# A graph and expert megakernel on one Trainium2 core: ten groups instead of six added back in the slots, another spacing of gathers and sorting steps, and attention's sum on GpSimd

## The chip, the cores and the metric

The kernel runs on 1 core of one Trainium2 chip. The metric is the device time in microseconds (us) of that core for one execution. The engines are named as in the profile: PE is TensorE's matmul, PEld its load of weights, DVE is VectorE, ACT is ScalarE, POOL is GpSimd and SP is SyncE, which here only issues DMAs.

## The reference

The input is `x`, 128 x 64 rows of 256 features (8192 tokens), with an adjacency matrix of 64 x 64 for each of the 128 graphs. Two layers follow one another, each with a part over the graph and a feed-forward part (FFN), and each part is added to `x`:

```python
x = x + _L0_gnn_ref(_layernorm(x), adj, ...)
x = x + _L0_ffn_ref(_layernorm(x), ...)
x = x + _L1_gnn_ref(_layernorm(x), adj, ...)
x = x + _L1_ffn_ref(_layernorm(x), ...)

def _L0_ffn_ref(...):                       # one expert of eight for each token
    H = gelu(xf @ W1 + b1)                  # 1024 hidden features
    probs = softmax(H @ Wg + bg); assign = argmax(probs)
    for e in range(8):
        y = H @ Wd[e] + bd[e]
        out = out + where(assign == e, probs[:, e] * y, 0.0)

def _L1_gnn_ref(...):                       # attention inside each graph
    Wh = h @ W
    e = leaky_relu((Wh @ a1)[:, :, None] + (Wh @ a2)[:, None, :], 0.2)
    attention = softmax(where(adj > 0, e, NEG))
    h_prime = attention @ Wh
    return gelu(layernorm(h_prime) * gamma + beta)
```

The first graph part is a convolution with the normalised adjacency and a softplus. The last FFN takes gates from attention over 1,048,576 edges (a softmax of all the edges that end in a token), chooses 2 of 4 experts with them, and runs experts of 512 hidden features. Everything is float32 at the borders.

## The kernel before, in words

The 8192 tokens are 64 tiles of 128 tokens by 256 features, and they stay in SBUF as `x` (128 x 64 x 256, one tile is `x[:, t, :]`). Four tiles make a group (`GR = 4`), two groups a part (`PART = 2`). The program is written as generators that are advanced in turn, and a scheduler fixes the order of the instructions on each engine when the program is built: it takes what is ready by its own estimate, and `tc.issue_after(i)` holds what is emitted under it back until instruction `i` has its place. `reuse_waits="tile"` makes the next user of a buffer wait for the users of the one before.

The stages, by the profiled execution:

- *0 to about 655 us*: the first graph part and the hidden features of the first FFN. The tokens are ordered by their expert, and their hidden rows are written to DRAM in that order (`hrows`).
- *Slots, 655 to 918* (`slots`, from L1297 on, and the loop L1399 to L1413). A slot is 128 tokens of one expert. SP issues a DMA transpose that loads its hidden rows as `hTt`; TensorE adds the bias with a first matmul (L1340) and multiplies with 8 pieces of the expert's weights as 16 instructions (L1348); ScalarE copies the result from PSUM (L1356) and sends it to DRAM (`yrows`, L1357). The loop runs 60 slots.
- Beside each slot the loop advances three generators. `counts` (`Keys.count`, L328) counts the edges by the token that they end in: VectorE makes a pair of one-hot arrays with one comparison each (L209, 128 x 2048 and 128 x 1024 elements) and TensorE multiplies them into `cnt_ps` (L348). `steps` (`Keys.finish`, L360) sorts the edges' keys on VectorE in small steps, and each `next(steps)` takes one. `back_early` (`back_first`, L1268) adds the FFN's rows back to `x`: GpSimd gathers the 128 rows of a tile from `yrows` into `yearly` (L1285, an indirect DMA; five buffers, `HELD + 2`), and after `HELD` = 3 more gathers VectorE multiplies the tile by its probability and adds it to `x` (L1276), then takes the statistics for the next layernorm (L1277, bn_stats). The gather of tile `t` is emitted once the number of slots done reaches that in L1282; which slots hold a tile's rows depends on the data, so it waits for the stores emitted before it. When a part's eight tiles are in, `factors_of` (L245) makes the layernorm's scale and mean for the parts that attention needs first.
- *Attention, 920 to 1246* (loop L1733 to L1769, steps `s` = 4 to 25, a group advances by one stage in a step). The streams of a step are `back` (L1563: four gathers L1569 into `yin`, additions L1584, statistics L1561), `combine` (L1669), `tables` (L1687), `second` (L1642) and `first` (L1604), and each works on another group: group `s - 4` has its scores made in `first` (transposes, matmuls, `ee` at L1627), group `s - 5` its softmax and product in `second`, group `s - 7` is finished in `combine`, and group `s - 10` gives its rows for the edges in `tables`. `back` runs for `s >= BACKED` alone, since the groups below were added in the slots; their statistics come from `raws1`. After each second step `make_factors` (L1715) turns the statistics of the two groups that were added back, of the two rows of products and of the two finished groups into factors.
- The order of `back` in attention: the additions L1584 of groups 2 to 4 wait for a place behind the last factors, those of groups 5 to 8 behind the last scores, and later ones are free (`ahead` in `back`). Its `yin` buffers (six) are also those of the experts' `y`.
- `combine` ends with two instructions of VectorE for each tile (L1674, L1675), a gelu of the whole group on ScalarE (L1679, 128 x 1024), the sum `x + gelu` on VectorE (L1682, 128 x 1024) and the statistics of the sum for the last layernorm. There are 16 of each. Expert units of the last FFN (L1490 and L1500) fill in from `s` = 12 on.
- *1246 to 1951*: the edges' softmax and gates, and the experts, with matmuls of TensorE nearly throughout.

GpSimd also copies while the first stage runs (L598, 64 x 256 elements), which the prediction uses for its price, as it does the short `guess` instructions of VectorE (L163).

Of the kernel before, what the change touches and what calls it, by code (L numbers as in the profile page):

```python
# [17 lines left out]
ALU = mybir.AluOpType  # L18
# [9 lines left out]
PART = 2  # L28
# [6 lines left out]
SURE = 68  # L35
EARLY = 8
AHEAD = 3
BACKED = 3 * PART
HELD = 3
COUNTED, HE = 6, 8  # L40
EPS = 1e-5
# [46 lines left out]
def kernel(  # L88
# [31 lines left out]
    nc = tc.nc  # L120
    V, S = nc.vector, nc.scalar
    FD = f0_w1.shape[1]
    NH = FD // P
    E0 = f0_wg.shape[1]
# [109 lines left out]
    def factors_of(raw, eps, work, fac):  # L234

        sm, df, ve, y, w = work
        moments(raw, sm, df, ve)
        if eps is None:
            V.tensor_scalar(ve, ve, EPS, None, ALU.add)
        else:  # L240
            V.tensor_tensor(ve, ve, eps, ALU.add)
        scale = fac[:, 0]
        root_of_bits(scale, ve, y, w)
        last = V.scalar_tensor_tensor(fac[:, 1], sm, -0.5, scale, ALU.mult, ALU.mult)
        V.tensor_scalar(fac[:, 2], sm, 0.5, None, ALU.mult)  # L245
        return last.ins
# [215 lines left out]
    with tc.tile_pool(name="w0", bufs=1, reuse_waits="tile") as w0, tc.tile_pool(name="kp", bufs=1, reuse_waits="tile") as kp:  # L462
# [30 lines left out]
        with tc.tile_pool(name="bg1", bufs=1, reuse_waits="tile") as bg1, tc.tile_pool(  # L493
# [20 lines left out]
            with tc.tile_pool(name="b2", bufs=1, reuse_waits="tile") as b2, tc.tile_pool(  # L514
# [493 lines left out]
                for i in range(n_parts + 2):  # L1008
                    next_found(i + 1)

                    def factors():
                        ahead = look(i + 2, i + 1) if i + 2 < n_parts else iter(())
                        yield
                        next(ahead, None)
                        yield
                        make(i)
                        yield
                        for _ in ahead:
                            yield
# [228 lines left out]
        if True:  # L1248
            with tc.tile_pool(name="bs", bufs=3, reuse_waits="tile") as bs, tc.tile_pool(
# [18 lines left out]
                def back_first():  # L1268

                    held = []  # L1270

                    def add():
                        t, y = held.pop()
                        i, part = t % (PART * GR), t // (PART * GR)
                        raw = raws1[part]
                        V.scalar_tensor_tensor(x[:, t, :], y, psel[:, t : t + 1], x[:, t, :], ALU.mult, ALU.add)  # L1276
                        V.bn_stats(raw[:, 0, i, :], x[:, t, :])  # L1277
                        if i == PART * GR - 1 and part in facs:
                            facs["last"] = factors_of(raw, None, [m[:, None, :] for m in mfs], facs[part])

                    for t in range(BACKED * GR):
                        while done < E0 - 1 + 2 * t:  # L1282
                            yield
                        y = be.tile([P, D], F32, name="yearly")
                        got = nc.gpsimd.indirect_dma_start(  # L1285
                            y, None, yrows, bass.IndirectOffsetOnAxis(ap=row_y[:, t : t + 1], axis=0)
                        )
                        gathers.append(got.ins)
                        held.insert(0, (t, y))
                        if len(held) > HELD:  # L1290
                            add()
                    while held:
                        yield
                        add()
# [98 lines left out]

                raws1 = [c0.tile([P, 1, PART * GR, 6], F32, name=f"raw_{i}") for i in range(BACKED // PART)]
                for i in range(FIRST // PART):
                    facs[i] = c0.tile([P, 3, 1, PART * GR], F32, name=f"fac_{i}")
                mfs = [c0.tile([P, PART * GR], F32, name=f"mf_{i}") for i in range(5)]
                more, back_early, last = weights(), back_first(), None
                for t, unit in enumerate(slots(0, SURE - EARLY)):  # L1399
                    done = t  # L1400
                    with tc.issue_after(compared[0]) if t else ExitStack():
                        next(back_early, None)
                    with tc.issue_after(last) if last is not None else ExitStack():
                        next(counts, None)
                        if t % 2 == 0 or t % 8 == 3:
                            next(steps, None)
                    if t >= SURE - EARLY - 8:
                        next(more, None)
                    last = unit
# [129 lines left out]
    with ExitStack() as of_c:  # L1539
# [20 lines left out]
        def raw_stats(norm, k, src):  # L1560
            V.bn_stats(made["raw"][:, norm, s % PART * GR + k, :], src)  # L1561
# [107 lines left out]
        def combine(g):  # L1669
            hp = ring[:, g % RING]  # L1670
            hn = cz.tile([P, GR, D], F32, name="z")
            for k in range(GR):
                scale, _, mean = factors(g, 1, k)
                V.scalar_tensor_tensor(hn[:, k, :], hp[:, k, 0:D], mean, gam1, ALU.subtract, ALU.mult)  # L1674
                V.scalar_tensor_tensor(hn[:, k, :], hn[:, k, :], scale, bet1, ALU.mult, ALU.add)  # L1675
                if k == 1:
                    yield
            yield
            S.activation(hn, hn, AF.Gelu)  # L1679
            yield  # L1680
            xs = x[:, GR * g : GR * g + GR, :]
            V.tensor_tensor(xs, xs, hn, ALU.add)  # L1682
            for k in range(GR):
                raw_stats(2, k, x[:, GR * g + k, :])
            yield
# [47 lines left out]
        for s in range(FIRST, n_steps):  # L1733
            if s % PART == 0:
# [3 lines left out]
                V.memset(made["eps"], EPS)  # L1738
                if s < BACKED:
                    V.tensor_copy(made["raw"][:, 0], raws1[s // PART][:, 0])  # L1740
            streams = []
            for of, by_steps in ((back, 0), (combine, COMBINE), (tables, TABLES), (second, SECOND), (first, FIRST)):
                if 0 <= s - by_steps < NG and (of != back or s >= BACKED):
                    streams.append((of(s - by_steps), 2 if of == second and s % 2 else 0))
# [837 lines left out]
```

## Time and profile before

| what | us |
|---|---|
| median of six runs | 1959.23 |
| the six runs | 1955.28 to 1967.73 |
| the profiled execution's own time | 1953.44 |
| its span in the trace | 1951.7 |
| busy: PE, DVE, ACT, POOL | 1837.8, 1357.4, 919.4, 438.8 |
| slots, until the jump behind them | 655 to 918 |
| one slot from 812 on | 4.05 |
| one gather L1285 on GpSimd, one L1276, one L1277 on VectorE | 0.99, 0.479, 0.423 |
| sixteen L1682, each | 1.225 |
| attention, until the start of the edges' stage (L1787) | 920 to 1246 |

The span counts from the first to the last instruction of the trace; the device time is a little longer. Busy time is the time in which an engine executed something; an engine that is 94% busy over the whole is still idle in some stages, so a stage is read by itself, with the busy time of each engine against the stage's length. The granted clock is the share of its full speed that TensorE was given. In rows of groups the numbers behind a colon are the shortest, the median and the longest duration in ns and then the first and last start in us; in rows of single instructions they are start and duration in us, and the bracket at the end is the idle time of the engine just before and what ended it.

### The profile page before, as it was taken

The numbers are of one execution on the slowest core, as the hardware profiler recorded it, in microseconds if no ns is written. First come the engines' busy times: TensorE is split into PE (matmuls) and PEld (weight loads), VectorE is DVE, ScalarE is ACT, GpSimd is POOL, SyncE is SP. The second block draws the span as 40 slices with busy tenths as digits, with TensorE's granted clock in tenths as the row PEclk, the third lists the DMA queues.
The fourth block names the chain that finished last, engine by engine and source line by source line (L and its number), as shares of the span: only waits on it lengthen the run. The fifth ranks groups of instructions, "written<-read, shape, count | busy, mean of one in ns | idle before, by whom it ended". The sixth has DMA issues, their size and how long they took to land. (4 is left out here: it accounts for less than half of the span.)

```text
span 1951.7 us, 31223 instructions
## 1 busy us (share of the span) xinstructions
PE 1837.8 (94%) x10125; PEld 1280.6 (66%) x10125; DVE 1357.4 (70%) x4472; ACT 919.4 (47%) x1612; POOL 438.8 (22%) x465
## 2 busy tenths in 40 slices
PE   7899999999999999999879999989999999999998
PEld 5455555544556787787546676656666768888885
DVE  7788898885767999876787766757777542334435
ACT  4877887877652000001776775423333424333332
POOL 3011111010101010111221000036566632303214
PEclk9999999999999999999979999999999999999999
DMA  9762313242417987796133111842222348978943
GB/s 294 205 191 92 109 68 122 79 163 74 171 47 178 172 168 144 157 186 132 40 125 95 49 66 57 238 135 55 60 55 55 99 168 256 308 233 281 290 139 120
DMA packets 365895, 276.97 MB, mean 142 GB/s; under 512 B 195464, under 2 KB 327456, under 8 KB 365728
## 3 DMA queue, kind: packets, MB, share of 16 engines
q1 hardware_dynamic: 320896, 204.41, 38.2%
q0 software_dynamic: 23040, 60.22, 9.4%
q10 hardware_dynamic: 21792, 10.27, 2.1%
q8 instruction: 86, 1.41, 0.3%
q14 instruction: 81, 0.66, 0.1%
HBM read 115.91 MB, written 123.18 MB: 123 GB/s over the span
## 5 line engine op out<-in xcount | busy, mean ns | idle before, releaser
L505 PE MATMUL ph<-zT,w 128*128 128x512 f32 x512 | 248.5, 611 | 6.1 <-ACT hT L509 6.1
L1348 PE MATMUL py<-wd,hTt 128*128 x960 | 224.0, 388 | 0.0
L1348 PEld LDWEIGHTS py<-wd,hTt 128*128 128x128 f32 x960 | 182.1, 195 | 24.8 <-issue 0.2
L1963 POOL DMA_INDIRECT got<-tsrc,esrc x144 | 153.3, 1065 | 179.1 <-DMA zslots<-none 75.6
L1500 PE MATMUL py<-w,hT 128*128 128x256 f32 x736 | 173.6, 388 | 9.7 <-DVE td L2322 5.0
L1490 PE MATMUL ph<-zT,w 128*128 128x512 f32 x368 | 170.7, 607 | 0.0
L1500 PEld LDWEIGHTS py<-w,hT 128*128 128x128 f32 x736 | 138.2, 192 | 36.6 <-issue 13.0
L1356 ACT COPY y<-py 128x256 f32<-128x256 f32 x60 | 22.3, 372 | 284.1 <-PE py L1348 284.1
L872 POOL DMA_INDIRECT hrows<-rows,pos x64 | 65.4, 1021 | 396.0 <-ACT wd L654 75.0
L2444 ACT ACTIVATE hT<-ph,b1e 128x256 f32<-128x256 f32 x152 | 71.8, 473 | 171.4 <-PE ph L2440 90.5
L505 PEld LDWEIGHTS ph<-zT,w 128*128 128x128 f32 x512 | 90.5, 193 | 83.4 <-issue 72.9
L1494 ACT ACTIVATE hT<-ph,b 128x512 f32<-128x512 f32 x92 | 63.1, 687 | 173.7 <-PE ph L1490 147.2
L2440 PE MATMUL ph<-zTp,w1e 128*128 128x256 f32 x608 | 137.5, 379 | 0.7 <-ACT zTp L2422 0.7
L2453 PE MATMUL py<-w,hT 128*128 x608 | 137.5, 379 | 0.0
L2461 DVE TENSOR_TENSOR y<-py,b2e 128x256 f32<-128x256 f32 x76 | 32.2, 424 | 150.5 <-PE py L2453 127.5
L668 PE MATMUL pre<-wd 128*128 128x512 f32 x256 | 126.8, 608 | 2.1 <-ACT wd L654 1.3
L2440 PEld LDWEIGHTS ph<-zTp,w1e 128*128 128x128 f32 x608 | 115.4, 190 | 16.6 <-ACT zTp L2422 0.9
L509 ACT ACTIVATE hT<-ph,b 128x512 f32<-128x512 f32 x128 | 87.9, 688 | 81.2 <-PE ph L505 73.5
L808 ACT COPY rows<-tz 128x1024 uint16<-128x1024 uint16 x112 | 110.2, 1020 | 26.5 <-DMA hrows<-rows,pos 17.3
L2453 PEld LDWEIGHTS py<-w,hT 128*128 128x128 f32 x608 | 112.6, 190 | 13.8
L1490 PEld LDWEIGHTS ph<-zT,w 128*128 128x128 f32 x368 | 68.2, 193 | 68.2 <-issue 67.4
L807 PEld LDWEIGHTS tz<-ident,hT 128*128 128x128 f32 x512 | 60.8, 142 | 73.6 <-ACT rows L808 35.1
(505 smaller groups left out, 3754.2 us busy)
## 6 DMA issues: line engine op xcount, KB each, us to landing
w1e<-in_L_ffn_W_dram SPq DMA_DIRECT2D x38, 512.0 KB
yin<-ystore SPq DMA_DIRECT2D x24, 512.0 KB
yrows<-none SPq DMA_DIRECT2D x10, 1024.0 KB
zslots<-none SPq DMA_DIRECT2D x38, 256.0 KB
zin<-zslots SPq DMA_DIRECT2D x38, 256.0 KB
yslots<-y SPq DMA_DIRECT2D x76, 128.0 KB
ystore<-y SPq DMA_DIRECT2D x72, 128.0 KB
x<-in_x_dram SPq DMA_DIRECT2D x8, 1024.0 KB
```

What stands on the lines that cost most here:

```text
L505: nc.tensor.matmul(ph, w1[:, c, q * P : q * P + P], zT[:, c, :], start=(c == 0), stop=(c == 1))
L509: gelus.append(S.activation(hT, ph, AF.Gelu, bias=b1[:, q : q + 1]).ins)
L668: nc.tensor.matmul(pre, xnT[:, c, n * P : n * P + P], wcat[:, c, :], start=(c == 0), stop=(c == 1),)
L808: copy(rows[:, :, :, q * P : q * P + P], th.bitcast(U16).rearrange("p (k n h) -> p k h n", k=GR, h=2),)
L872: nc.gpsimd.indirect_dma_start(hrows.rearrange("(r h) f -> r (h f)", h=2), bass.IndirectOffsetOnAxis(ap=pos[:, t : t + 1], axis=0), rows[: ...
L1348: nc.tensor.matmul(py, hT[:, q, :], wd[:, bass.ds(e, 1), q, :].rearrange("p e f -> p (e f)"), start=False, stop=(q == NH - 1),)
L1490: nc.tensor.matmul(ph, w1[:, e, c, q * P : q * P + P], zT[:, c, :], start=(c == 0), stop=(c == 1))
L1500: nc.tensor.matmul(py, hTs[q][:, k * P : k * P + P], w2[:, e, q, :], start=(q == 0), stop=(q == NH1 - 1))
L1963: nc.gpsimd.indirect_dma_start(got, None, tsrc, bass.IndirectOffsetOnAxis(ap=esrc[:, b, at : at + 1], axis=0))
L2440: nc.tensor.matmul(ph, w1e[:, c, q * P : q * P + P], zT[:, c, :], start=(c == 0), stop=(c == 1))
L2444: pace[:] = [S, S.activation(hT, ph, AF.Gelu, bias=b1e[:, q : q + 1]).ins]
L2453: nc.tensor.matmul(py, hTs[q][:, k * P : k * P + P], w2[:, e, q, :].rearrange("p e f -> p (e f)"), start=(q == 0), stop=(q == NH1 - 1),)
```

## The change

Four edits. The constant `BACKED` goes from six groups to ten, so that 40 tiles instead of 24 are gathered and added back beside the slots, and attention's `back` runs for groups 10 to 15 alone; `raws1` grows from three tiles of statistics to five. A gather is emitted once `t * 8 // 7` slots behind the first seven are done, where it was `2 * t`: seven gathers in eight slots instead of one in two. The sorting steps are taken in three of eight slots for the first 24 slots and in seven of eight behind them, where they were taken in five of eight throughout. The sum `x + gelu` of `combine` goes from VectorE to GpSimd.

```diff
-BACKED = 3 * PART
+BACKED = 5 * PART
...
                     for t in range(BACKED * GR):
-                        while done < E0 - 1 + 2 * t:
+                        while done < E0 - 1 + t * 8 // 7:
                             yield
...
-                        if t % 2 == 0 or t % 8 == 3:
+                        if t % 8 in (0, 3, 5) if t < 3 * E0 else t % E0 != E0 - 1:
                             next(steps, None)
...
             xs = x[:, GR * g : GR * g + GR, :]
-            V.tensor_tensor(xs, xs, hn, ALU.add)
+            nc.gpsimd.tensor_tensor(xs, xs, hn, ALU.add)
             for k in range(GR):
                 raw_stats(2, k, x[:, GR * g + k, :])
```

`E0` is 8.

## The prediction

> **What bounds the kernel now.** I read the page's forty slices first, to find the stages that are not filled by TensorE.
>
> ```profile
> PE   7899999999999999999879999989999999999998
> DVE  7788898885767999876787766757777542334435
> PEclk9999999999999999999979999999999999999999
> ```
>
> A slice is 48.8 us. TensorE has 8 or 9 tenths nearly everywhere; it is weak at the start, in slices 19 and 20 (928 to 1025 us, where its clock falls too) and at 1270 us. Slices 13 to 15 (634 to 780) have a full VectorE beside a full TensorE. The change touches the slots (655 to 918) and the attention stage (920 to 1246), so I cut these by their own events: the slots at the start of slot 11 (700.3) and slot 34 (812.2), attention where the factors of a pair of steps begin.
>
> ```profile
> 655.00:700.30 45.30, 45.30 (x344) 39.31 (x343) 44.39 (x108) 4.05 (x11) 0.99 (x1) 0.96 0.93 185
> 700.30:812.20 111.90, 101.77 (x764) 85.65 (x761) 109.00 (x324) 8.55 (x24) 15.01 (x12) 0.95 0.75 154
> 812.20:917.60 105.40, 105.40 (x868) 92.14 (x864) 75.65 (x160) 9.73 (x27) 11.84 (x11) 1.00 0.83 166
> ...
> 943.90:1029.10 85.20, 66.06 (x303) 43.95 (x303) 76.05 (x255) 60.83 (x116) 27.02 (x25) 0.84 0.33 102
> 1029.10:1199.90 170.80, 166.27 (x850) 114.45 (x849) 112.91 (x366) 121.68 (x218) 8.04 (x11) 1.00 0.19 62
> 1199.90:1245.80 45.90, 45.90 (x272) 29.69 (x273) 39.38 (x170) 19.20 (x36) 0.17 (x1) 1.00 0.54 178
> ```
>
> Columns: stretch, length, then busy time of PE, PEld, DVE, ACT and POOL, granted clock, DMA share, GB/s. From 812 on a slot takes exactly 4.05 us (the bias matmuls of L1340 start 4.05 apart) and TensorE is never idle: TensorE binds. From 700 to 812 the 23 slots take 111.9 us where 23 x 4.05 = 93.2 would do; VectorE is busy 109.0 of 111.9, and the waits name it:
>
> ```profile
> PE cnt_ps L348 <- DVE one L209: 8.9, 10, 2.0
> ```
>
> So VectorE binds there and costs 18.7 us. It binds again from 944 to 1029 (76.05 of 85.2), where TensorE is busy 66 at a clock of 0.84. After 1029 TensorE binds (166.3 of 170.8, then all of 45.9).
>
> **The change part by part.** The trace gives durations; for the changed program I read the order of its instructions on each engine, which no clock enters.
>
> *Slots.* 16 more tiles are gathered by GpSimd and added by VectorE. Each costs an L1276 (0.479) and an L1277 (0.423), 0.90 us, so 14.4 us in all. The rule for the sorting steps was meant to make room by moving steps to later slots. The order shows that it hardly does: between the first nine pairs of one-hots (L209, one pair a slot) the same sorting operations stand as before, since the scheduler takes them as soon as they are ready, and by pair 34 the same ones are done as before. The adds come instead at pairs 9, 10, 11, 12, 14 and so on: 23 up to pair 34 where 12 were. VectorE gets 11 x 0.90 = 9.9 us more to do before pair 35, or 8.0 by start-to-start times (0.73 an add). Before, it was saturated to the end of pair 33 (812.4); pair 34 then took 2.6 and pair 35 could have started at 815.0. It will start at 823.0 to 824.9, its one-hots take 1.9 and its sixteen matmuls 0.65: 825.6 to 827.5. TensorE reached that point at 820.3 + 4.05 = 824.3. That is 1.3 to 3.2 late; with slower matmuls after gaps (the clock is 0.95 there) I take **+4**. From pair 36 on a slot asks VectorE for 2.5 us of 4.05, and the rest of the adds hides; pairs 47 to 49 ask 15 to 16 us of 12.2, which the two pairs that VectorE may run ahead (8.1 us) take up. Bounds: 0 (all hidden) and 14.4 (nothing hidden). Below 0 is excluded: no operation leaves this stage. The gathers themselves: in before an add runs some 21 us behind its gather.
>
> ```profile
> 692.25 0.99 POOL L1285 DMA_INDIRECT yearly<-yrows,row_y  x1 [71.16 <-DMA hTt<-hrows]
> 713.93 0.48 DVE L1276 SCALAR_TENSOR_TENSOR x<-yearly,psel,x 128x256 f32<-128x256 f32 x1
> ```
>
> Now it runs two or three slots (8 to 12 us) behind the slot that the gather waits for, and a gather starts 8.2 us after that slot's start; where DVE is not late it will wait a few us for the landing, with slack to spare. Behind a waiting gather only gathers are queued on GpSimd. SP's queue is unchanged.
>
> *Start of attention.* Groups 10 to 12 have no order point to wait for (before, groups 6 to 8 waited for made scores). Their 12 gathers and 12 additions stand at the head of both queues, before the first scores L1627, which now follow an idle time:
>
> ```profile
> 931.65 0.42 DVE L1627 TENSOR_TENSOR ee<-p,wh 128x256 f32<-128x256 f32 x1 [10.54 <-ACT wh L1614]
> ```
>
> Gathers start every 1.26 us from 920.16; the twelfth at 934.0, it lands 2.4 later, its addition takes 0.48: 936.9. So the 10.5 us of idleness take the additions in, but the scores come 5.3 late. The exponentials behind them stand in ScalarE's queue ahead of three copies that free PSUM for TensorE, so I carry **+4** of it on, between +2 (recovered by the next wait) and 5.3.
>
> *944 to 1029.* VectorE loses 26 additions (L1584, two in 0.87: 0.43 each, 11.2), 14 statistics of groups 6 to 9 (two in 0.74: 5.2) and 5 additions of gelus (L1682, 1.22: 6.1): 22.5 of 76.05. GpSimd's addition of 128x1024 is not in the trace. From below, VectorE's 1.22; from above four of GpSimd's slowest copy of 256 elements, 4 x 0.833 = 3.3.
>
> ```profile
> L598 POOL COPY wd<-wd x32: 387/398/833, 6.8 to 275.7; 64x256 f32<-64x256 f32 x32
> L163 DVE SCALAR_TENSOR_TENSOR guess<-work,guess x26: 129/178/419, 19.7 to 1564.5; 128x32 f32<-128x32 f32 x22, 128x16 f32<-128x16 f32 x4
> ```
>
> Nearest is the usual copy, 4 x 0.45 = 1.8 for one input; two inputs are between that and 3.3, and I take 2.5. VectorE has the statistics of the sum next in its queue, for group 0 only three operations (1.1) behind the last input of the gelu: gelu 1.06 + 2.5 + 0.2 - 1.1 = 2.6 of waiting, against 0.9 before; other groups have 8 to 10 operations of cover. I charge 1.2 for each of the five: 6. VectorE keeps 53.6 + 6 = 60. ScalarE loses four table loads in this stretch by the new order (of 10; in the whole stage 27 stand where 33 were), 4 x 1.28 of 60.8: 55.7. TensorE's 66 at clock 0.84 are 55.5 at full clock. The busiest is at 60; handoffs made 85.2 of 76.05 (1.12), which gives 67, and a clock not quite recovered makes me take 71.5: **-13.7** (from -5, if the clock and the chain stay, to -18).
>
> The second row above says something else: the longest L163, at 20.54, ran 0.42 instead of 0.18 beside a GpSimd copy (20.52 for 0.40), to the copy's very end. [...]
>
> *After 1029.* TensorE has 4.5 us of idleness in 171; I take **-1.5** (0 to -4). In the last 46 us TensorE is always busy and the last three additions are 1.3 (2.5 - 1.22) later each: 0, at worst +4. The later gathers of groups 13 to 15 stand behind the additions of groups 0 to 6 on GpSimd and ahead of 7's; the order leaves them room in both directions, so 0.
>
> Sum: +4 +4 -13.7 -1.5 = **-7.2 us**. The profiled execution took 1953.44 (span 1951.7), which is 5.8 under the median of the six runs, 1959.23. I put the same change to the median: **1952.0**.
>
> **The rivals.**
> [...]
> - *VectorE binds the slots harder*: the place is pairs 9 to 35, full already (109.0 of 111.9). If the nearer gathers land late (7.5 us was the longest landing here, 2.4 the shortest), the additions stall a VectorE that has no slack. Price: the whole 14.4 of additions on the path; with attention at -13.7 + 4 + 4 it ends at +9, **1968**. It decides once the slots lose over 13 us or attention's gain stays under 8. Against it: from 812 on a third of VectorE is free.
> - *The spreading does what it says*: steps leave the full stretch and the 18.7 us shrink by the room that 812 to 918 has. That would give -10 in the slots and 1938. The order, unchanged in the first nine pairs, speaks against it; under 0.05, inside the first case's chance.
>
> **How the numbers follow.** 0.3% (5.9 us) is about what a measurement of this kernel can tell from no change. Forecast 0.42 (with the third rival; its own range 1940 to 1953), handoffs 0.30, slots 0.28. The range runs from forecast with the best bounds (-18 in the stretch, +2 and 0 elsewhere: about -19, 1940) to the second rival with some excess, 1971. Faster 0.42, same 0.30, slower 0.28.
>
> **What would show it.** Slots: slot 37 four us later against slot 11, then 4.05 again; VectorE 97% busy to 825. Attention: first L1627 about 17 us after the first gather; the stretch between the factors of steps 5 and 11 at 71 in place of 85; clock over 0.9 in it; L1682 on POOL near 2.5. Wrong: a stretch over 80, or slots that lose over 10 or gain.

## The result and the profile after

The changed kernel takes 1971.17 us (median of 20 runs, 1961.84 to 1984.10) where before, over 46 runs now, takes 1958.54. The ratio is 1.0066 with a 95% interval of 1.0050 to 1.0082: **12.9 us slower**, where 7 us faster was forecast.

The profiled execution of the changed kernel took 1975.45 (span 1973.7), 22.0 more of span than before. Cut at the same events, the difference falls into these parts ("slot 4" is the first bias matmul L1340 of the loop; "factors" are the L245 of a pair of steps):

| stretch | before | after | difference | forecast |
|---|---|---|---|---|
| start to slot 4 | 671.9 | 679.6 | +7.7 | 0 |
| slot 4 to the first gather of attention | 248.3 | 250.3 | +2.0 | +4 |
| first gather to the factors of step 5 | 23.7 | 31.2 | +7.5 | +4 |
| factors of step 5 to those of step 11 | 85.2 | 75.3 | -9.9 | -13.7 |
| factors of step 11 to the end of attention | 216.7 | 228.2 | +11.5 | -1.5 |
| end of attention to the end | 705.9 | 709.1 | +3.2 | 0 |

Up to slot 4 both programs have the same order of instructions on every engine; the other kernels of this study, with that same order, reach slot 4 at 671.4 to 681.6, so the 7.7 is not the change's. The same holds for the last row, which lies between 682 and 713 in the kernels below. The four rows between them make +11.1, near the 12.9 of the ratio.

The forty slices of the changed kernel's page:

```profile
PE   7899999999998998999789999989899999999998
DVE  7789898885677999976586666756787452334435
PEclk9999999999999999999889999999899999999999
```

A slice is 49.3 us. VectorE is full to slice 16 where it was full to 15, which is the additions of ten groups in the slots, and emptier in slices 19, 21 and 22. TensorE is weaker in slices 12, 15, 19 and 28, and in 20 stronger. The stretches of the changed kernel, cut at slot 11, slot 34, and attention's first gather and factors (stretch, length, busy PE, PEld, DVE, ACT, POOL, clock, DMA share, GB/s):

```profile
663.30:708.00 44.70, 44.70 (x342) 38.82 (x341) 44.08 (x108) 4.04 (x11) 1.94 (x2) 0.96 0.88 184
708.00:819.40 111.40, 99.23 (x765) 83.32 (x762) 109.22 (x340) 8.56 (x24) 22.65 (x20) 0.98 0.74 164
819.40:927.40 108.00, 106.35 (x871) 92.46 (x868) 83.60 (x176) 9.73 (x27) 20.77 (x18) 1.00 0.83 171
929.90:961.10 31.20, 23.93 (x94) 15.46 (x94) 13.14 (x41) 15.71 (x36) 11.53 (x12) 0.84 0.22 60
961.10:1036.40 75.30, 61.91 (x305) 41.72 (x304) 59.47 (x210) 54.41 (x113) 11.72 (x5) 0.91 0.22 71
1036.40:1215.50 179.10, 169.36 (x850) 114.97 (x849) 113.26 (x358) 118.82 (x216) 30.41 (x20) 0.99 0.20 62
1215.50:1264.60 49.10, 47.48 (x272) 29.41 (x273) 39.36 (x167) 19.32 (x36) 7.91 (x6) 1.00 0.49 169
```

The slots from 708 to 819 last what they lasted (111.4 against 111.9) with 16 instructions more on VectorE. From 961 the relief shows: VectorE is busy 59.5 where it was 76.1, and the clock is 0.91. The loss is in the last two rows. TensorE, which had 4.5 us of idleness there and none in the last 46, has 9.7 and 1.6, although VectorE's busy time is what it was (113.3 and 112.9 in the first of the two rows). The rest of the loss is TensorE's own busy time, 216.8 over the two rows where it was 212.2. So what has to be explained is a stage in which VectorE has room and TensorE waits all the same.

The first scores come as late as was forecast. VectorE's rows of the changed kernel:

```profile
934.18 0.88 DVE L1584 SCALAR_TENSOR_TENSOR x<-yin,psel,x 128x256 f32<-128x256 f32 x2 [3.04 <-DMA yin<-yrows,row_y]
...
946.64 0.49 DVE L1584 SCALAR_TENSOR_TENSOR x<-yin,psel,x 128x256 f32<-128x256 f32 x1 [0.84 <-DMA yin<-yrows,row_y]
947.04 0.42 DVE L1627 TENSOR_TENSOR ee<-p,wh 128x256 f32<-128x256 f32 x1
```

Twelve additions follow twelve gathers, eight of them after a wait for the gather (10.2 us in all), and the first scores stand right behind the last, 17.1 us after the first gather; it was 11.5.

The sum on GpSimd, by its line in the changed kernel (shortest, median, longest in ns), and who waited for it (us, times):

```profile
L1682 POOL TENSOR_TENSOR x<-x,z x16: 2342/2356/2572, 970.5 to 1245.5; 128x1024 f32<-128x1024 f32 x16
...
  DVE raw L1561: 18.4, 7
```

And one of the sixteen close up, VectorE first, then GpSimd, then TensorE:

```profile
1095.25 0.73 DVE L1460 TENSOR_SCALAR z<-x,fac 128x256 f32<-128x256 f32 x2
1096.46 2.16 DVE L1662 SCALAR_TENSOR_TENSOR eps<-ring 128x4 f32<-128x4 f32 x1 [0.49 <-ACT ring L1658]
1098.55 0.41 DVE L1561 BATCH_NORM_STATS2 raw<-ring 128x6 f32<-128x256 f32 x1
1098.88 0.39 DVE L1460 TENSOR_SCALAR z<-x,fac 128x256 f32<-128x256 f32 x1
1099.20 1.39 DVE L1561 BATCH_NORM_STATS2 raw<-x 128x6 f32<-128x256 f32 x4
1100.51 0.39 DVE L1460 TENSOR_SCALAR z<-x,fac 128x256 f32<-128x256 f32 x1
1100.83 0.41 DVE L1627 TENSOR_TENSOR ee<-p,wh 128x256 f32<-128x256 f32 x1
```

```profile
1096.25 2.35 POOL L1682 TENSOR_TENSOR x<-x,z 128x1024 f32<-128x1024 f32 x1 [10.16 <-ACT z L1679]
```

```profile
1101.29 1.13 PE L1490 MATMUL p<-zT,w 128*128 128x512 f32 x2 [1.49 <-DVE ee L1627]
```

L1662 handles 128 x 4 numbers. Its sixteen instructions in the kernel before and in the changed one:

```profile
L1662 DVE SCALAR_TENSOR_TENSOR eps<-ring x16: 147/158/167, 942.8 to 1208.0; 128x4 f32<-128x4 f32 x16
```

```profile
L1662 DVE SCALAR_TENSOR_TENSOR eps<-ring x16: 147/165/2176, 960.2 to 1223.6; 128x4 f32<-128x4 f32 x16
```

In the close-up it begins 0.21 behind GpSimd's sum and lasts 2.16, to 1098.62; the sum ends at 1098.60. Everything behind it in VectorE's queue is 2 us late, the scores L1627 among it, and TensorE waits for the scores, whose PSUM buffer the expert's matmul takes next. A *hold* is called below what happened here, an instruction of VectorE that lasts to the end of a sum on GpSimd, and a *wait* is VectorE standing idle until a sum is done. There are nine holds in the changed kernel (15.9 us over the instructions' medians) and seven waits (18.4). Together VectorE loses 34.3 us to sums of which it has been relieved; its own sixteen took 16 x 1.225 = 19.6, with 8.8 us of standing idle for the gelu in front of them.

The trace also shows the way from VectorE to TensorE. Of the 11.3 us that TensorE is idle in the last two rows, 7.6 end with an instruction of VectorE (L1627, L1504, L1460 or L159), in eight gaps; seven of these end 1 to 4 us behind the end of a sum that had held VectorE or kept it waiting. In the kernel before, no gap does.

### The profile page after: what moved, and what is told of

Read it like the earlier page. It is cut to its first block, busy times and chain, and to the rows that moved or that the text cites. A ratio compares the mean times of both kernels' runs of the same rounds, so it can differ in the third digit from the quotient of the medians.

```text
span 1973.7 us, 31223 instructions
## 1 busy us (share of the span) xinstructions
PE 1843.1 (93%) x10125; PEld 1279.4 (65%) x10125; DVE 1355.1 (69%) x4458; ACT 910.0 (46%) x1606; POOL 479.0 (24%) x481
## 5 line engine op out<-in xcount | busy, mean ns | idle before, releaser
L505 PE MATMUL ph<-zT,w 128*128 128x512 f32 x512 | 250.6, 615 | 6.2 <-ACT hT L509 6.2
L1500 PE MATMUL py<-w,hT 128*128 128x256 f32 x736 | 175.6, 391 | 10.8 <-DVE kt L1902 4.9
L807 PEld LDWEIGHTS tz<-ident,hT 128*128 128x128 f32 x512 | 61.1, 143 | 73.8 <-ACT rows L808 36.1
```

The lines of the kernel that those rows point to most:

```text
L505: nc.tensor.matmul(ph, w1[:, c, q * P : q * P + P], zT[:, c, :], start=(c == 0), stop=(c == 1))
L1500: nc.tensor.matmul(py, hTs[q][:, k * P : k * P + P], w2[:, e, q, :], start=(q == 0), stop=(q == NH1 - 1))
```

## The experiments

The theory after the result: two faults. The sum on GpSimd gets in VectorE's way; and twelve additions ahead of the first scores make attention start late. Rival: the loss comes from the order that ten groups give, and the sum is harmless. The first four kernels separate the edits. Later runs were made on other chips, where before took 1939.65 and 1941.09, so the ratio to before is compared, with its 95% interval, and a difference in us is the ratio's. Stages are read from one profile of each kernel, cut at events rounded to 0.1 us.

**The sum alone** (the kernel before with the last edit):

```diff
-            V.tensor_tensor(xs, xs, hn, ALU.add)
+            nc.gpsimd.tensor_tensor(xs, xs, hn, ALU.add)
```

> Only attention's sum x + gelu goes to GpSimd; slots and groups as before. Theory (hold): the addition on GpSimd takes 2.35 us and VectorE's instructions with two inputs in SBUF that meet it last until its end (nine in the changed kernel, 15.9 us in all), and the statistics of the sum wait for it besides; VectorE is relieved of 16 x 1.22 = 19.6 us, which is worth something only from 944 to 1029. Expected 3 to 8 us slower than before, with the loss after 1029 us. Rival (order): the loss after 1029 comes from the order that the ten groups give, the sum on GpSimd is harmless: 0 to 5 us faster than before.

Measured: 1.0084 (1.0053 to 1.0116), 16.5 us slower: the rival falls, and the theory's 3 to 8 is too small. In its profile the sums hold VectorE for 22.7 us and it waits 12.5 for them. The stretch of 85.2, where relief was to show, takes 89.4.

**The groups alone** (the changed kernel with this line as before):

> The changed kernel with the sum x + gelu back on VectorE, so ten groups in the slots and the new spacing alone. Theory (hold): the 11.6 us lost after the factors of step 11 go away, the slots keep +2, the late first scores +6 to +7, and the stretch from the factors of step 5 to those of step 11 still gains 6 to 10 of its 85: within 3 us of before, 8 to 12 us faster than the changed kernel. Rival (order): about as slow as the changed kernel, 10 to 16 us over before, since VectorE gets 19.6 us of sums back.

Measured: 1.0044 (1.0015 to 1.0073), 8.6 us slower. The 11.5 lost behind the factors of step 11 are gone (216.0 against 216.7 of before), as the theory said; but the start takes 36.1 from the first gather to the factors of step 5, and the stretch gains 6.9. The start costs more than the theory had, but not all of the 36.1 is the additions' (see "The sum in four pieces").

**The hold alone** (the kernel before, and GpSimd adds once more into the spent buffer):

```diff
             V.tensor_tensor(xs, xs, hn, ALU.add)
+            nc.gpsimd.tensor_tensor(hn, xs, hn, ALU.add)
```

> The kernel before, with 16 further additions of 128 x 1024 on GpSimd that nobody reads (into the spent buffer of the gelu, behind VectorE's own sum), so that only the hold is added and no result waits. Theory (hold): each lasts 2.35 us and about half of them stretch a VectorE instruction with two inputs in SBUF to their own end: some 16 us of stretching, 3 to 10 us slower than before. Rival (waiting): the hold costs nothing beside TensorE, only the statistics' wait for the sum does: no change, within 2 us.

Measured: 1.0058 (1.0034 to 1.0081), 11.4 us slower; attention is 7.5 longer in the profile. Nothing waits for these additions, yet they cost: 3.3 us between the factors of step 5 and those of step 11, and 4.2 behind them (220.9 against 216.7). They hold VectorE for only 6.5 us, since the statistics that ran beside them were not held (nine statistics beside a sum in the changed kernel took 0.41 to 0.43 us, where the median is 0.41); well under the expected 16. This is the cleanest of the experiments: throughout attention all other instructions stand in the order of before on every engine, but for two neighbours on VectorE that have changed places. Moving the sum itself also makes the scheduler order other instructions anew (in the sum alone, some 140 of VectorE's 796 in attention stand elsewhere), and no run keeps that order while the sum moves.

**The groups with a place** (the sum on VectorE, ten groups, and an order point for groups 10 to 12, whose additions had none):

```diff
-            elif FIRST < g <= 2 * FIRST:
+            elif BACKED <= g < BACKED + 3:
                 ahead = made["scores"]
```

> The kernel of ten groups with the sum on VectorE, and the additions of groups 10 to 12 given a place behind the last scores, as groups 6 to 8 had before. Theory: the first scores come about 11.5 us after the first gather in place of 17, the stretch behind them keeps its gain, and it is 4 to 7 us faster than the same kernel without the order point, 2 to 6 faster than before. Rival (recovered anyway): the late scores are made up inside the stretch, and it is the same as without the order point within 2 us.

Measured: 0.9975 (0.9952 to 0.9998), 4.9 us faster than before and 13.5 faster than the same groups without a place. The first scores stand 10.8 behind the first gather again. Attention takes 318.7, before 325.6. The first gather starts at 926.88, and VectorE's row of the first scores is:

```profile
937.66 0.42 DVE L1627 TENSOR_TENSOR ee<-p,wh 128x256 f32<-128x256 f32 x1 [9.53 <-PE p L1618]
```

**All four edits, with that place**:

> The changed kernel whole, with the sum on GpSimd, and the additions of groups 10 to 12 given a place behind the last scores. Theory (two faults that add): the sum on GpSimd costs what it cost alone, 10 to 17 us, and the late start is gone, so 10 to 17 us over the ordered kernel with the sum on VectorE and 5 to 13 over before. Rival (one fault): the sum hurts only a stage that is late already, and this is as fast as the ordered kernel with the sum on VectorE, 2 to 6 us faster than before.

Measured: 1.0043 (1.0026 to 1.0060). Against the ordered kernel with the sum on VectorE that is 0.68%, 13 us: the sum costs as much where attention starts on time, and the rival falls. But the faults do not simply add: alone they make 16.5 and 8.6, together 12.9.

**The sum in four pieces** (the changed kernel):

```diff
-            nc.gpsimd.tensor_tensor(xs, xs, hn, ALU.add)
+            for k in range(GR):
+                nc.gpsimd.tensor_tensor(xs[:, k, :], xs[:, k, :], hn[:, k, :], ALU.add)
```

> The changed kernel with the sum on GpSimd cut into four additions of 128 x 256. Theory (length of the hold): each can hold VectorE for 0.6 us instead of 2.35, and the statistics of the first tile can start after the first piece; 3 to 8 us faster than the changed kernel. Rival (GpSimd's total time): the pieces take 2.4 us together and hold as much; within 2 us of the changed kernel, 10 to 15 over before.

Measured: 1.0051 (1.0032 to 1.0070), not told apart from the changed kernel's 1.0066. The hold went, and it did not help. This kernel's line of the sum and who waited for it:

```profile
L1683 POOL TENSOR_TENSOR x<-x,z x64: 717/727/935, 971.3 to 1244.7; 128x256 f32<-128x256 f32 x64
...
  DVE raw L1561: 23.2, 55
```

Three instructions are held, for 0.7 us in all instead of 15.9; but VectorE now waits 23.2 for the pieces, 55 times, where it waited 18.4.

This profile also shows what the late start costs by itself. From the first gather to the factors of step 5 the kernel has the order of the changed kernel and of the groups alone on TensorE, VectorE and ScalarE; ScalarE stands idle 4.9 us for the late scores, and the stretch takes 30.2, 6.5 more than before. The 31.2 of the changed kernel and the 36.1 of the groups alone hold something else besides, which is told under "What stays open".

**Gathers doubled** (the ordered kernel, sum on VectorE):

```diff
                 ys.append(y)
+            if g < BACKED + 2:
+                for k in range(GR):
+                    nc.gpsimd.indirect_dma_start(ys[k], None, yrows, ...)   # the same rows again
```

> The ordered kernel (sum on VectorE, additions behind the scores) in which the gathers of groups 10 and 11 are issued twice into the same buffers, so that twelve gathers run at the head of attention as in the changed kernel, but no addition stands before the first scores. Theory (burst): in the changed kernel TensorE's transposes finished only when the row of gathers was through, so the first exponentials come 4 us or more later than in the ordered kernel and the whole is 4 to 10 us slower than it. Rival (place of the additions): the twelve additions ahead of the first scores are the cause, and this is within 2 us of the ordered kernel.

Measured: 0.9974 (0.9964 to 0.9985), the same as the ordered kernel; the first scores come 10.4 behind the first gather although twelve gathers follow one another from 933.66 on (this kernel's L1633 is L1627 of the others):

```profile
944.10 0.42 DVE L1633 TENSOR_TENSOR ee<-p,wh 128x256 f32<-128x256 f32 x1 [9.19 <-PE p L1624]
```

The burst falls: it is the additions ahead of the scores that make attention late.

**Twelve groups** (the ordered kernel with `BACKED = 6 * PART` and a gather every `t * 9 // 8` slots):

> The ordered kernel with twelve groups in the slots in place of ten (nine tiles gathered per eight slots of the old count: t * 9 // 8 slots behind the first seven). Theory: additions hide in the slots from slot 34 on (VectorE was busy 76 of 105 us there), so 8 tiles more cost nothing there and take 0.9 us each off attention, of which a third shows: 0 to 4 us faster than the ordered kernel. Rival: the slots are full and pay 0.9 us for each: up to 7 us slower than it.

Measured: 0.9973 (0.9960 to 0.9986), as ten. Both sides were right in part: the slots take 256.1 (ten groups: 249.0 to 254.6; six: 248.3 to 250.6) and attention 313.4 (ten: 318.7).

**Statistics behind the scores** (all four edits and the place; the statistics of the sum are taken out of `combine` and emitted at the end of the step):

```diff
+            if "summed" in made:
+                g2 = made.pop("summed")
+                with tc.issue_after(made["scores"]):
+                    for k in range(GR):
+                        raw_stats(2, k, x[:, GR * g2 + k, :])
```

> The changed kernel with groups 10 to 12 ordered behind the scores, the sum whole on GpSimd, and the four statistics of the sum put behind the scores of their step in VectorE's queue, so that no scores stand behind a wait for the sum. Theory (wait): the cost of the sum on GpSimd is VectorE's wait for it ahead of the next scores; it goes, and from the factors of step 11 to the end of attention it takes under 219 us in place of 226; 2 us faster than before to 3 slower. Rival (hold): additions of 2.35 us hold VectorE as often as they did; 224 us or more in this stretch and 6 to 11 us over before.

Measured: 1.0023 (1.0011 to 1.0035). The stretch from the factors of step 11 takes 225.3, which is the hold's number, while the total is 4 us better than with the statistics ahead (the two intervals overlap). VectorE's waits in this kernel:

```profile
DVE raw L1561 <- POOL x L1682: 3.4, 1, 3.4
```

The waiting has nearly gone (15.8 in the kernel without this edit), and the holding has grown from 16.7 to 24.7 us, 14 instructions, among them the scores' own L1633, L1635 and L1638. What does not wait is held.

**The same in four pieces**:

> The same with the sum on GpSimd in four pieces of 128 x 256, which held VectorE for 1.5 us in all where whole sums held it for 16. Wait theory: the same time as with the whole sum behind the scores, within 3 us. Rival (hold): 5 us or more faster than with the whole sum.

Measured: 1.0006 (0.9994 to 1.0018), 3.3 us better than the whole sum behind the scores: between the two numbers, and the intervals overlap. 9.5 us of hold and 4.1 of waiting are left, and the stretch still takes 222.4.

**The same with the sum on VectorE**, ten groups and twelve:

> The ordered kernel of ten groups with the sum on VectorE and the statistics of the sum behind the scores: what the place of the statistics does by itself. Wait theory: a sum on VectorE ends 1.2 us before its statistics and nothing waits, so within 3 us of the ordered kernel, 2 to 8 us faster than before. Rival (place): statistics behind the scores bring the scores forward for any sum, and it is over 3 us faster than the ordered kernel.

> Twelve groups in the slots, additions of the later groups and statistics of the sum behind the scores, the sum on VectorE: the version that the runs so far point to. Expected 4 to 9 us faster than before, as the kernel of twelve groups alone or up to 3 us better.

Measured: 0.9956 (0.9939 to 0.9972) with ten, 8.5 us faster than before and the lowest ratio of all; 0.9966 (0.9953 to 0.9979) with twelve, not told apart from it. Against the ordered kernel's 0.9975 on another chip, ten groups with the statistics behind the scores are not clearly better, so the rival (place) stays open.

By now three ways of arranging the sum on GpSimd all cost in the same stretch. Left were its length (2.35 for 1.22 us) and the second engine. The three kernels that follow add a sum or leave it out, so they no longer compute the same thing; each ran once and is read by stages. Their whole times were 1961.45, 1945.08 and 1944.43, beside 1960.44 for the kernel before on that chip.

**The sum twice on VectorE** (the ordered kernel; x gets the gelu two times):

> The ordered kernel of ten groups in which VectorE adds the gelu to x twice, one addition behind the other (so x gets the gelu two times), which makes each sum 2.45 us long as on GpSimd, with no second engine, no hold and no handoff. Read by stages, from the factors of step 11 to the end of attention, where it is 214 us with one sum on VectorE and 225 to 228 with the sum on GpSimd. Theory (length): each sum's added 1.2 us stands on the way from gelu to statistics to factors, so 223 to 228. Rival (two engines): VectorE has room here (113 of 171 us), and what costs is the hold and the handoff: 214 to 218.

Measured: 215.2, against 214.1 with one sum; length alone falls, as far as one profile tells. From the factors of step 5 to those of step 11 it takes 87.0 against 81.8, so there VectorE's time counts. One line each of the ordered kernel with the sum on VectorE, with the sum on GpSimd, and with two sums on VectorE, from the factors of step 11 to the end of attention:

```profile
1031.50:1245.60 214.10, 211.41 (x1118) 143.72 (x1119) 152.08 (x534) 139.74 (x252) 10.37 (x13) 1.00 0.26 85
```

```profile
1041.30:1267.40 226.10, 215.17 (x1120) 143.14 (x1119) 154.08 (x527) 137.41 (x251) 38.54 (x26) 1.00 0.25 81
```

```profile
1039.80:1255.00 215.20, 212.51 (x1118) 144.01 (x1119) 164.72 (x545) 141.80 (x254) 11.40 (x13) 1.00 0.25 82
```

Two sums make VectorE 12.6 us busier (fourth number behind the stretch: 164.72 against 152.08), and TensorE stays idle for 2.7 us as with one. With one sum on GpSimd VectorE is hardly busier and TensorE is idle for 10.9.

**No sum**, in the ordered kernel and in the kernel before:

> The ordered kernel of ten groups without the sum x + gelu (attention's result is left out of x): the most that taking the sum off VectorE could ever bring. By stages: the prediction's step gives 4 to 7 us less from the factors of step 5 to those of step 11 (82 us) and nothing behind them. If VectorE's time is not what binds there, under 2 us less.

> The kernel before without the sum x + gelu (attention's result is left out of x). From the factors of step 5 to those of step 11 (85 us, VectorE 76 busy): the prediction's step takes five sums of 1.22 and their handoffs out, 5 to 8 us less. If the chain of handoffs binds, under 3 us less.

Measured: 74.0 in place of 81.8, and 77.2 in place of 85.2, from the factors of step 5 to those of step 11; 217.8 and 217.0 behind them, no gain (214.1 and 216.7 with the sum). So relief of VectorE is worth 8 us in that stretch, and nothing after; in the ordered kernel 3.7 of the 8 are lost again behind it. The kernels with the sum on GpSimd get at most 3 of these 8: 75.3 against 78.3 without the place, 81.7 against 81.8 with it, and 89.4 against 85.2 in the old order.

The sum on GpSimd in all its forms, from the factors of step 11 to the end of attention:

| kernel | hold, us | wait, us | stretch | with the sum on VectorE |
|---|---|---|---|---|
| changed | 15.9 | 18.4 | 228.2 | 216.0 |
| sum alone | 22.7 | 12.5 | 227.6 | 216.7 |
| all edits with the place | 16.7 | 15.8 | 226.1 | 214.1 |
| in four pieces | 0.7 | 23.2 | 225.4 | 216.0 |
| statistics behind the scores | 24.7 | 3.4 | 225.3 | 216.0 |
| both | 9.5 | 4.1 | 222.4 | 216.0 |

(Hold and wait are over the whole of attention.) TensorE's idle time in this stretch that ends with an instruction of VectorE is 5.0 to 8.9 us in these six kernels. In the kernels with one sum or two on VectorE it is 0 to 0.5, but for twelve groups with the statistics behind the scores (2.4); in the hold alone it is 1.3.

## Why the prediction was wrong, step by step

- **What bounds**: right. VectorE binds from 944 to 1029; without the sum 8 us go there and none behind.
- **Slots, +4**: right in kind, half in size. The program asked for 9.9 us more of VectorE before pair 35; the stage grew by 2.0 in the changed kernel and by 1.9 in the mean of eleven profiles with ten groups against four with six (251.8 and 249.9). Slot 37 stands 125.1 us behind slot 11 where it stood 124.1 behind, not four us later as written. The order showed that the new rule for the sorting steps does little: with the old rule in place of it, one instruction of VectorE stands a few places later and no engine's order is otherwise different. No run was made of that.
- **Start, +4**: the mechanism is the one described (17.1 us to the first scores, "about 17" was written). The lateness carried on is 7.5, not 4, of which the additions explain 6.5 by the kernel in four pieces. It is the step with the cheapest repair: the place for groups 10 to 12 turns +8.6 into -4.9.
- **Stretch to the factors of step 11, -13.7**: -9.9. The clock rose to 0.91 as said. Part of this gain is not relief but additions done earlier, at the start; with them in their place the stretch takes 81.7 to 81.8, with the sum on either engine.
- **The sum's price**: the duration was 2.36 where 2.5 was taken, but the step charged 1.2 us for five sums and nothing for the other eleven. That is **the term that failed**: "After 1029 ... I take -1.5" and "the last three additions are 1.3 later each: 0". Measured +11.5, and 9 to 12 against the same kernel with the sum on VectorE in the four kernels that have the whole sum on GpSimd. The reasoning was that TensorE binds there and VectorE has room (113 of 171). But an instruction that is stopped by a sum stands in VectorE's queue in front of the scores, which run in order behind it, and the room comes too late for TensorE: it was idle 7.6 us for VectorE in the changed kernel and not at all in the kernel before. Two sums on VectorE cost 1.1 us in the same room.
- **The row that spoke against the change**, a 0.42 us L163 that lasts to the end of a GpSimd copy, was the right sign: nine instructions of the changed kernel last to the end of a sum in the same way. The forecast put no time to it.
- **The rivals**: 1968 was named for "VectorE binds the slots harder". The time is near, the mechanism is not: the slots lost 2, not 13. Additions did wait for late gathers there (10.1 us), but all of them behind 850 us, where VectorE has slack. As for handoffs (0.30): what cost was VectorE held by the sums and waiting for them, 34.3 us in the attention of the changed kernel, and the loss came behind the factors of step 11 (+11.5), not in the stretch before them (-9.9). The lower end of the range is -16 by the bounds as written, or -20 with the -4 after 1029, and not -19, which does not bear on the miss.

What stays open: how the cost divides into holding, waiting and the changed order of the other instructions. The hold alone, in the old order, cost 4.2 in the stretch for 6.5 us of holding; each experiment that took holding or waiting away raised the other, and 13.6 us of both together still cost 6.4. Also open is a part of the late start: in the kernel of the groups alone ScalarE's second pair of copies L1601 waited 9.6 us, until 950.00, for transposes that the trace puts at 939.1 to 940.2 (5.3 us, until 946.92, in the changed kernel). The gathers doubled do not bring that, nor does the kernel in four pieces, which has the same additions and the same order there, so it isn't shown to belong to the change.

## What to carry to other kernels

The elementwise sum moved from VectorE to GpSimd was not taken off VectorE here, where the instructions beside it read two tensors of SBUF: VectorE lost 28 to 35 us to sixteen sums that last 38 on GpSimd and 20 on VectorE. Price such a move by the sum's whole length on GpSimd, once for each place where it occurs, as an upper bound of what VectorE loses (here 38 against those 28 to 35), and look at what stands behind it in VectorE's queue, not at VectorE's busy share. When work is done in an earlier stage, look at which order points went with it: here an `if` on group numbers no longer covered the groups that were left, and one line made the difference between slower and faster. What removing an operation could bring at most is a cheap experiment (leave it out), and it should be read by stages.

## What the runs showed of the hardware

- In four kernels with whole sums on GpSimd (changed, sum alone, hold alone, all edits with the place), 40 instructions of VectorE began while a sum ran (over 0.1 us before its end) and read two tensors in SBUF, or were the scaling L1460 (one tensor and scalars from SBUF): 39 lasted to the sum's end, within 0.3 us. The 40th, an L1674, began 0.2 behind the sum and kept its 0.48; that sum took 2.90 instead of 2.35. Of 104 others, statistics (77), a reduction, copies and sums that read PSUM, none was held: in the changed kernel nine statistics beside a sum took 0.41 to 0.43 us, a reduction L1637 0.40 and an L1504, which reads PSUM, 0.42. L1460 reads one tensor, as the statistics do, and was held all the same, five times out of five (2.13 us at 1246.05 in the changed kernel, where its median is 0.41); what sets it apart, no run shows. The start in the profile doesn't tell who is stopped: besides that L1674, an L1584 of the sum alone began 0.34 us ahead of a sum and still lasted to its end, 3.0 us in place of 0.48.
- 128 x 1024 added on GpSimd takes 2.356 us (median of the changed kernel), in four pieces 4 x 0.727 = 2.9; on VectorE 1.225. The prediction took 2.5 for GpSimd.
- In these runs the holds made a stage late without making VectorE look busier: its busy time from 1036 to 1215 is 113.3 with 9.6 us of holds in it and was 112.9 before, because the sums' own time (eight sums, 9.8 us) had gone from it.
